# A four-layer image network on one core: the last image's norm by blocks under its own scans, and its inverse DFT and token layers in interleaved parts

## The chip, the cores and the metric

The kernel runs on one NeuronCore of a Trainium2 chip. The metric is device time in microseconds (us): 12547.97 us is the median of three runs (12536.14 to 12569.25). The profile comes from one further execution. A difference of 0.3% either way is about what counts as no change.

## The reference

The input is four images of 64 x 64 positions and 96 channels. Layer 0 is a 2D selective-scan block (four scan directions), layer 1 is the same kind of block applied to the image's real 2D DFT, with real and imaginary parts as 192 channels on 64 x 33 frequencies, and layers 2 and 3 are token layers: linear attention and a feed-forward part quantized to fp8.

```python
x = x + ss2d_0(group_norm(x))            # layer 0: 96 -> 192 channels
xf = rfft2(x); x = x + irfft2(ss2d_1(xf))  # layer 1: 192 -> 384 channels
t = tokens(x)                            # 4096 tokens of 96
for l in (2, 3):
    t = t + attn_l(layer_norm(t))        # (q k^T) v, without a softmax
    t = t + ffn_l(layer_norm(t))         # operands rounded to fp8 e5m2, sums to fp16
```

```python
def ss2d(x):
    xin, z = split(x @ in_proj.T)
    u = silu(depthwise_conv3x3(xin) + b)
    for k in range(4):                   # rows, columns, and both reversed
        dt, B, C = split(x_proj[k] @ u_k)
        delta = softplus(dt_proj[k] @ dt + bias)
        h = h * exp(delta * A) + delta * u_k * B     # along the sequence, 16 states
        y_k = sum_n(C * h) + D * u_k
    y = layer_norm(merge(y_0, y_1, y_2, y_3)) * silu(z)
    return y @ out_proj.T
```

## The kernel before

Channels lie on the 128 partitions in three chunks (C = 3). Layer 0 treats two images at a time (two "pairs" of half-width channels), layer 1 one image at a time. The scans are written in `scans`: six phases in a row (pair 0, pair 1, then layer 1 of images 0 to 3), in each the directions 0, 2, 1, 3, in each direction segments of the sequence. Layer 0 has 8 segments of 512 positions. Layer 1 has segments of 512, 512, 384, 384 and 320 positions, which are blocks of 8, 8, 6, 6 and 5 rows; directions 2 and 3 run through them from the last to the first. A segment is 12 steps: four groups of four states, times three channel chunks. A phase of layer 1 is so 240 steps, 96 of them 512 wide, 96 of 384 and 48 of 320; 1728 steps in all.

A step issues, in an order written out by hand: two exponentials on ScalarE (`ax`, L551), transposes of `bx` by TensorE (L546), four `tensor_tensor_scan` on VectorE (`hx`, `hy`, L576), products with C on GpSimd (`hcx`, L722) and on VectorE (`hcy`, L740), and transposing accumulations by TensorE (`acc`, L598). When the last group of a segment's chunk is through, `close_chunk` copies `acc` to SBUF (L625) and stores it to `y` in DRAM (L627), one step later. Rows of C and B are fetched by SyncE (SP) three steps ahead, as broadcasts (`bc`).

All other work is written as Python generators, "side" work. Each step has three slots; in a slot at most one generator is resumed up to its next `yield`, so a piece of its instructions goes into the engines' streams between those of the scan. `rate` of the phase (RATES) is the mean number of resumptions per step. A generator that yields LATE is only resumed in the third slot, before `hcy`. Work put off with `E.defer` (mostly the copy out of PSUM) is issued at the next slot. In the scans the side work has one PSUM buffer (`ms`).

The side lists: pair 1's preparation under phase 0; norm and out_proj of pair 0 with DFT and projection of images 0 and 1 under phase 1, and so on; `end1` of image b (norm, out_proj, inverse DFT, token layers) under the scans of image b + 1. `end1` of image 3 runs alone after the scans (`alone`, four PSUM buffers), outside of the hand-written order. What a list has left over goes on into the next phase; what is left after the last step is run by `E.finish`.

The parts of `end1`:

- `gated`: by blocks of rows, loads `y` of all directions (`yt`, L300, L304) and `u` (`ut`, L306), two rows at a time, merges and transposes them in PSUM (`py`, L327, L333), takes means and variances by matmuls (`pm` L347, `pv` L357), scales, multiplies with the gate and projects (`out1`, `po` L831), storing `att`.
- `inverse`: three groups of 32 channels in a row. Each loads `at` (L912), does 128 matmuls `piv` (L920, L921) and their copies to `v`, then 16 matmuls `pio` (L934), adds the image and stores `x1` (L940).
- `tokens`: loads all tokens (`tok`, L960) and the layer's weights, then a pipelined `layer_norm` over all tokens, the Gram matrix `pg` (L1036) and a chain of small matmuls, attention in 8 groups of four token columns (`pt` L1057, `pao` L1063), `layer_norm`, and the feed-forward in 8 groups (`ptf` L1072, `ph` L1080, `h16` and `h8` L1081 to L1087, `pfo` L1092, y16 L1100 to L1106). `h16`, `h8` and `y16` have one buffer.

Of the kernel before, what the change touches and what calls it, by code (L numbers as in the profile page):

```python
# [6 lines left out]
F32 = mybir.dt.float32  # L7
F16 = mybir.dt.float16
F8 = mybir.dt.float8e5
AF = mybir.ActivationFunctionType  # L10
# [15 lines left out]
RATES = [1.4, 2.25, 2.47, 2.47, 2.47, 2.47]  # L26
# [30 lines left out]
class Env:  # L57
# [5 lines left out]
    def __init__(self, tc, psum):  # L63
        self.tc, self.nc, self.psum = tc, tc.nc, psum
        self.later, self.queue, self.done = [], [], set()
        self.key = self.task = self.wants = None
# [44 lines left out]
class Block:  # L111
# [171 lines left out]
    def gated(self, E, g, io, out_proj):  # L283
# [5 lines left out]
        with E.pool(f"{cfg.pre}nm{g}") as sp:  # L289
# [4 lines left out]
                (b, i, r + i, min(2, n - i)) for b, (r, n) in enumerate(cfg.rows) for i in range(0, n, 2)  # L294
# [14 lines left out]
            todo = iter(tiles)  # L309
            nxt = load(*next(todo))  # L310
            yield
            yield
            yield
            for b, (r, nr) in enumerate(cfg.rows):
                n = nr * 64
                nm = f"{cfg.pre}_{g}_{r}"
# [3 lines left out]
                for i in range(0, nr, 2):  # L320
                    m = min(2, nr - i) * 64
                    yt, ut = nxt
                    more = next(todo, None)
                    nxt = load(*more) if more else None
# [81 lines left out]
def scans(tc, ctx, phases, ident):  # L406
# [213 lines left out]
    def close_chunk(st):  # L620

        z, c = st.z, st.c
        y = sp.tile([P, NBK, P], F32, name=f"y_{st.nm}", tag="y", bufs=2)
        for lo, hi, n in z.runs:
            nc.scalar.copy(y[:n, lo:hi], z.acc[c][:n, lo:hi])  # L625
            t = z.a + lo * P
            nc.sync.dma_start(  # L627
                out=z.ph.io["y"][z.k % 2][z.k // 2, t : t + (hi - lo) * n, c * P : (c + 1) * P].rearrange(
                    "(b p) d -> p b d", p=n
                ),  # L630
                in_=y[:n, lo:hi],
            )
# [266 lines left out]

def inverse(E, cst, att, x, b, x1):  # L900

    nc = E.nc
    G = 32
    with E.pool(f"fi{b}") as sp:
# [4 lines left out]
        for c0 in range(0, CH, G):  # L909
            a = sp.tile([HH, WF, 2, G], F32, name=f"at_{b}_{c0}", tag="at")  # L910
# [4 lines left out]
            v = sp.tile([WF, G, 2, HH], F32, name=f"v_{b}_{c0}", tag="v")  # L915
# [10 lines left out]
            HC = 16  # L926
            for h0 in range(0, HH, HC):
                xr = sp.tile([WW, HC, G], F32, name=f"xr1_{b}_{c0}_{h0}", tag="xr", bufs=2)
# [13 lines left out]
                )  # L942
        yield
# [5 lines left out]
def tokens(E, ins, consts, ident, x1, b, out):  # L949


    nc = E.nc
    A = CH + 1
    with E.pool(f"tk{b}") as sp:
# [3 lines left out]
        nc.sync.dma_start(out=mask, in_=consts["head_mask"])  # L958
        x = sp.tile([P, NT, CH], F32, name=f"tok_{b}", tag="tok")
        nc.sync.dma_start(out=x, in_=x1.rearrange("(p t) c -> p t c", t=NT))  # L960
        xn = sp.tile([P, NT, A], F32, name=f"xn_{b}", tag="xn")
        nc.gpsimd.memset(xn[:, :, CH:A], 1.0)
        yield
        yield

        def layer_norm(nm):

            Q = 8
            parts = []

            def scale(part, ts):
                t0, v = part
                for t in ts:
                    nc.scalar.activation(xn[:, t0 + t, :CH], xn[:, t0 + t, :CH], AF.Copy, scale=v[:, t : t + 1])  # L974

            n = NT // Q
            for i in range(n + 2):
                yield LATE
                if 1 <= i <= n:
                    nc.vector.tensor_reduce(parts[i - 1][1], sq, AX.X, ALU.add)  # L980
                if i < n:
                    t0 = i * Q
                    s = sp.tile([P, 2, Q], F32, name=f"lns_{nm}_{t0}", tag="lns", bufs=3)
                    m = s[:, 0, :]
                    parts.append((t0, s[:, 1, :]))
                    xs, xq = x[:, t0 : t0 + Q, :], xn[:, t0 : t0 + Q, :CH]
                    nc.vector.tensor_reduce(m, xs, AX.X, ALU.add)
                    nc.vector.tensor_scalar(m, m, 1.0 / CH, None, ALU.mult)
                    nc.vector.tensor_tensor(
                        xq, xs, m.rearrange("p (t o) -> p t o", o=1).to_broadcast([P, Q, CH]), ALU.subtract  # L990
                    )
                if i >= 2:
                    scale(parts[i - 2], range(4, Q))
                if i == n + 1:
                    return
                yield
                if i < n:
                    sq = sp.tile([P, Q, CH], F32, name=f"lnq_{nm}_{t0}", tag="lnq", bufs=2)
                    nc.scalar.activation(sq, xq, AF.Square)
                if i >= 1:  # L1000
                    v = parts[i - 1][1]
                    nc.scalar.activation(v, v, AF.Ln, bias=eps, scale=1.0 / CH)
                    nc.scalar.activation(v, v, AF.Exp, scale=-0.5)
                    scale(parts[i - 1], range(4))
# [6 lines left out]

        for ly in (2, 3):
            nm = f"{b}_{ly}"
            wq = sp.tile([A, 3 * CH], F32, name=f"wqkv_{nm}", tag="wqkv")
            nc.sync.dma_start(out=wq, in_=ins[f"l{ly}_wqkv"])
            wqt = sp.tile([CH, A], F32, name=f"wqt_{nm}", tag="wqt")
            nc.sync.dma_start(out=wqt, in_=ins[f"l{ly}_wqt"])
            wff = sp.tile([CH, CH], F32, name=f"wff_{nm}", tag="wff")
            nc.sync.dma_start(out=wff, in_=ins[f"l{ly}_wff"])
            bff = sp.tile([A, CH], F32, name=f"bff_{nm}", tag="bff")  # L1020
            nc.sync.dma_start(out=bff, in_=ins[f"l{ly}_bff"])
            q = {}
            for name, shape in (("w1", [CH, 4 * CH]), ("w2", [P, 3, CH]), ("b1", [P, 3]), ("b2", [P, CH])):
                t = sp.tile(shape, F32, name=f"{name}_{nm}", tag=name)
                src = ins[f"l{ly}_{name}"]
                nc.sync.dma_start(out=t, in_=src.to_broadcast([P, CH]) if name == "b2" else src)
                q[name] = sp.tile(shape, F8, name=f"q{name}_{nm}", tag=f"q{name}")
                yield LATE
                nc.vector.tensor_copy(q[name], t, saturate=False)
                if name in ("b1", "b2"):  # L1030
                    nc.vector.tensor_copy(t, q[name])
                    q[name] = t
            yield from layer_norm(nm + "a")
# [15 lines left out]
            small(CH, mt, wff, f"pw_{nm}", lambda t: nc.scalar.copy(pw, t))  # L1049
            yield  # L1050
            wo = sp.tile([A, CH], F32, name=f"wo_{nm}", tag="wo")
            small(A, wqt, pw, f"pe_{nm}", lambda t: nc.vector.tensor_tensor(wo, t, bff, ALU.add))
            yield
            for g in range(NT // 4):
                pt = E.psum(f"pt_{nm}_{g}")[:A]
                for i in range(4):
                    nc.tensor.transpose(pt[:, i * P : (i + 1) * P], xn[:, g * 4 + i, :], ident)  # L1057
                xt = sp.tile([A, 512], F32, name=f"xt_{nm}_{g}", tag="xt", bufs=2)
                E.defer(lambda xt=xt, pt=pt: nc.scalar.copy(xt, pt))
                yield  # L1060
# [233 lines left out]
```

## Time and profile before

| what | us |
|---|---|
| median of three runs | 12547.97 |
| the profiled execution | 12570.44 |
| its span, first to last instruction | 12568.7 |
| start to first scan step's end | 531 |
| scans, six phases | 2505, 2621, 1548, 1559, 1636, 1586 |
| after the last scan step | 580 |

| engine | busy us | share of the span |
|---|---|---|
| VectorE (DVE) | 10484.0 | 83% |
| TensorE (PE) | 9890.4 | 79% |
| ScalarE (ACT) | 9119.7 | 73% |
| GpSimd (POOL) | 8877.6 | 71% |

The phases are taken from the start of the first `hcy` of each to that of the next. The shares are means over stretches with different limits, so the stretches are read one by one: a row of a windows view gives the start and end of a stretch, its length, each engine's busy time in it (with the number of instructions), the granted share of the TensorE clock, and the DMA's share and rate. A wait row gives an engine and instruction, what it waited for, total us, how often, and the longest.

### The profile page before, as it was taken

What the parts mean: (1) busy time and instruction counts of PE and PEld (TensorE: products, weight loads), DVE (VectorE), ACT (ScalarE), POOL (GpSimd) and SP (SyncE); (2) the same over time, 40 slices, a digit from 0 to 9 for tenths busy, and PEclk for the clock granted to TensorE, in tenths of its full rate; (3) what the DMA queues carried; (4) which work ended last, traced back from release to release, by engine and by line L of the source; (5) the groups of instructions that cost most, each with busy time, mean ns of one, the idle gap of its engine ahead of it and who ended that gap; (6) DMA issues with size and microseconds to landing.
All of it is one profiled execution on the core that took longest, in us unless ns stands there. A gap on an engine that the chain in (4) does not pass through costs nothing. (4 is left out here: it accounts for less than half of the span.)

```text
span 12568.7 us, 164814 instructions
## 1 busy us (share of the span) xinstructions
PE 9890.4 (79%) x54680; PEld 7002.8 (56%) x54680; DVE 10484.0 (83%) x10170; ACT 9119.7 (73%) x18624; POOL 8877.6 (71%) x7057
## 2 busy tenths in 40 slices
PE   4677777777788878778888788788778977888766
PEld 1355555555666556556665565555556555565544
DVE  1399999999999998998788888978989699897923
ACT  1488888888778888886667777766777577776723
POOL 0388889998878898887678777866668566675600
PEclk8789999998989998998889998988789788887875
DMA  4344444444555445445443443443234322442231
GB/s 122 107 131 124 125 123 127 125 123 123 150 147 121 126 129 129 130 124 149 142 122 116 126 118 124 145 113 97 82 107 141 88 87 82 140 120 83 82 85 26
DMA packets 1264705, 1464.40 MB, mean 117 GB/s; under 512 B 494243, under 2 KB 1027055, under 8 KB 1255143
## 3 DMA queue, kind: packets, MB, share of 16 engines
q1 hardware_dynamic: 1263847, 1453.85, 41.8%
q8 instruction: 430, 7.05, 0.2%
q14 instruction: 428, 3.51, 0.1%
HBM read 1217.05 MB, written 236.50 MB: 116 GB/s over the span
## 5 line engine op out<-in xcount | busy, mean ns | idle before, releaser
L569 POOL TENSOR_TENSOR hy_l<-du_l,bc_l 128x512 f32<-128x512 f32 (+2 forms) x3456 | 3956.2, 1165 | 2358.8 <-DVE hcy_l L740 1194.6
L722 POOL TENSOR_TENSOR hcx_l<-hx_l,bc_l 128x1024 f32<-128x1024 f32 (+2 forms) x1617 | 3525.5, 2180 | 250.0 <-DVE hx_l L576 217.2
L526 ACT ACTIVATE bx_l<-dut_l,bt_l 128x192 f32<-128x192 f32 (+2 forms) x6272 | 2770.9, 498 | 0.1
L598 PE MATMUL acc_l<-ident,hcy_l 128*128 128x128 f32 (+1 forms) x12006 | 1854.2, 303 | 395.5 <-DVE hcy_l L740 392.2
L598 PE MATMUL acc_l<-ident,hcx_l 128*128 128x128 f32 (+1 forms) x12006 | 1885.0, 306 | 327.5 <-POOL hcx_l L722 322.7
L551 ACT ACTIVATE ax_l<-delta_l,l_alog 128x512 f32<-128x512 f32 (+2 forms) x3456 | 2138.9, 666 | 0.0
L598 PEld LDWEIGHTS acc_l<-ident,hcy_l 128*128 128x128 f32 (+1 forms) x12006 | 1553.3, 156 | 928.6 <-DVE hcy_l L740 574.4
L598 PEld LDWEIGHTS acc_l<-ident,hcx_l 128*128 128x128 f32 (+1 forms) x12006 | 1541.1, 156 | 823.1 <-POOL hcx_l L722 598.8
L576 DVE TENSOR_TENSOR_SCAN hx_l<-ax_l,state_l,b_l 128x512 f32<-128x512 f32 (+2 forms) x1663 | 1804.2, 1126 | 218.9 <-PE b_l L546 136.8
L740 DVE TENSOR_TENSOR hcy_l<-hy_l,bc_l 128x1024 f32<-128x1024 f32 (+2 forms) x1617 | 1926.8, 1192 | 43.7
L576 DVE TENSOR_TENSOR_SCAN hy_l<-b_l,state_l,hy_l 128x512 f32<-128x512 f32 (+2 forms) x1664 | 1808.3, 1121 | 139.1 <-ACT b_l L551 119.8
L551 ACT ACTIVATE b_l<-delta_l,l_alog 128x512 f32<-128x512 f32 (+2 forms) x1928 | 1210.3, 628 | 820.2 <-DVE hx_l L576 774.3
L546 PE MATMUL b_l<-ident,bx_l 128*128 128x128 f32 (+1 forms) x6776 | 1208.4, 305 | 406.9 <-DVE hy_l L576 200.3
L551 ACT ACTIVATE ab_l<-delta_l,l_alog 128x512 f32<-128x512 f32 x1308 | 900.0, 688 | 664.8 <-DVE hx_l L576 622.1
L546 PEld LDWEIGHTS b_l<-ident,bx_l 128*128 128x128 f32 (+1 forms) x6776 | 838.0, 153 | 925.1 <-DVE hy_l L576 314.1
L576 DVE TENSOR_TENSOR_SCAN hy_l<-ab_l,state_l,hy_l 128x512 f32<-128x512 f32 x948 | 1160.2, 1259 | 74.2 <-ACT ab_l L551 71.5
L576 DVE TENSOR_TENSOR_SCAN hx_l<-ax_l,state_l,ab_l 128x512 f32<-128x512 f32 x949 | 1161.1, 1264 | 68.2 <-PE ab_l L546 27.1
L546 PE MATMUL ab_l<-ident,bx_l 128*128 128x128 f32 x5236 | 897.2, 307 | 380.3 <-DVE hy_l L576 177.2
L589 POOL COPY state_l<-hx_l 128x2 f32<-128x2 f32 x1344 | 1087.6, 809 | 0.0
L546 PEld LDWEIGHTS ab_l<-ident,bx_l 128*128 128x128 f32 x5236 | 650.4, 155 | 711.7 <-DVE hx_l L576 272.9
L244 PE MATMUL pc_l<-pad_l,l_dg 128*128 128x512 f32 (+2 forms) x1944 | 927.2, 577 | 83.5 <-ACT uh_l L233 73.8
L163 PE MATMUL pi_l<-xi_l,l_wi 96*128 96x384 f32 (+6 forms) x912 | 446.6, 674 | 280.0 <-DMA xi_l<-xn 136.4
(192 smaller groups left out, 12605.9 us busy)
## 6 DMA issues: line engine op xcount, KB each, us to landing
bc_l<-l_xd_l SPq DMA_DIRECT2D x1536, 256.0 KB
bc_l<-l_xd_l SPq DMA_DIRECT2D x384, 512.0 KB
bc_l<-l_xd_l SPq DMA_DIRECT2D x384, 384.0 KB
us_l<-l_u SPq DMA_DIRECT2D x96, 768.0 KB
l_y<-y_l SPq DMA_DIRECT2D x288, 256.0 KB
bc_l<-l_xd_l SPq DMA_DIRECT2D x192, 320.0 KB
yt_l<-l_y SPq DMA_DIRECT2D x264, 192.0 KB
yt_l<-l_y SPq DMA_DIRECT2D x128, 384.0 KB
```

The source lines that it names most:

```text
L163: self.nc.tensor.matmul(out[i * cfg.PI : (i + 1) * cfg.PI, :n], wi[:, ki, half, :], xin[:, max(i, ki), :n], start=(ki == 0), stop=(ki == c ...
L244: nc.tensor.matmul(pc[:, : n * 64].rearrange("p (r w) -> p r w", w=64), diag[:, t, :], pad[:, r - p0 + dy : r - p0 + dy + n, dx : dx + 64] ...
L526: nc.scalar.activation(t[:n, b, :, ch], z.dut[:n, b, :, ch], AF.Copy, scale=z.bt[:n, b, m : m + 1])
L546: nc.tensor.transpose(pb[:, t : t + n], st.z.bx[st.q, j][:n, b, st.c], ident[:n, :n])
L551: nc.scalar.activation(out, z.delta[:, st.c, : z.S], AF.Exp, scale=z.blk.A[:, st.c, z.k, n : n + 1])
L569: nc.gpsimd.tensor_tensor(st.hy[:, j, :S], st.z.du[:, st.c, :S], st.z.b[st.q][:, j, :S], ALU.mult)
L576: nc.vector.tensor_tensor_scan(h[:, j, : z.S][:, ::step], a[:, : z.S][:, ::step], b[:, : z.S][:, ::step], 0.0 if z.first else z.state[st.c ...
L589: copy(z.state[st.c][:, n0 : n0 + 2].rearrange("p (j o) -> p j o", o=1), h[:, :, e : e + 1])
L598: nc.tensor.matmul(z.acc[st.c][:n, b, :], hc[:, j, t : t + n], ident, start=(n0 + j == 0 and b == 0), stop=(n0 + j == NST - 1 and b == 0), ...
L722: nc.gpsimd.tensor_tensor(hcx[:, :, :S], hx[:, :, :S], z.c[q][0][:, :, :S], ALU.mult)
L740: nc.vector.tensor_tensor(hcy[:, :, :S], st.hy[:, :, :S], z.c[q][1][:, :, :S], ALU.mult)
```

## The change

Four things are changed.

- `gated` takes its blocks in a given order and asks `ready(b)` before it loads one. `norm1_last` is `gated` for image 3, blocks in reverse order, each ready when the last direction's three chunks of that segment are closed (`closed`, written by `close_chunk`). It is the last side task of the last phase.
- `end1` is split into `norm1` and the rest. In `alone`, with `wide=4` and eight PSUM buffers, `inverse` runs its three channel groups in turns (`together`), and `tokens` runs its norm, attention and feed-forward as four parts of eight token columns in turns, each part with its own buffers, up to its own store of the output. Under the scans `wide` is 1 and parts follow one another; the norms are by parts there too.
- The weights of both token layers are loaded ahead of the inverse DFT in `alone`.
- RATES rise from 2.25 to 2.45 in phase 1, from 2.47 to 2.85 in phases 2 to 4 and to 3.0 in phase 5.

```diff
-RATES = [1.4, 2.25, 2.47, 2.47, 2.47, 2.47]
+RATES = [1.4, 2.45, 2.85, 2.85, 2.85, 3.0]
...
-    def gated(self, E, g, io, out_proj):
+    def gated(self, E, g, io, out_proj, order=1, ready=lambda b: True):
...
-            for b, (r, nr) in enumerate(cfg.rows):
+            nxt = None
+            for b, (r, nr) in list(enumerate(cfg.rows))[::order]:
                 n = nr * 64
+                if nxt is None:
+                    while not ready(b):
+                        yield
+                    nxt = load(*tiles.pop(0))
+                    yield
+                    yield
+                    yield
...
-                    more = next(todo, None)
-                    nxt = load(*more) if more else None
+                    nxt = load(*tiles.pop(0)) if tiles and ready(tiles[0][0]) else None
...
     def close_chunk(st):
 
         z, c = st.z, st.c
+        z.ph.io["closed"].append((z.k, z.a))
...
+def together(tasks, width):
+
+    tasks, active = list(tasks), []
+    while tasks or active:
+        while tasks and len(active) < width:
+            active.append(tasks.pop(0))
+        for task in list(active):
+            try:
+                yield next(task)
+            except StopIteration:
+                active.remove(task)
...
 def inverse(E, cst, att, x, b, x1):
...
-        for c0 in range(0, CH, G):
-            a = sp.tile([HH, WF, 2, G], F32, name=f"at_{b}_{c0}", tag="at")
+        def channels(c0, w):
+            a = sp.tile([HH, WF, 2, G], F32, name=f"at_{b}_{c0}", tag=f"at{w}")
...
+        W = min(E.wide, CH // G)
+        yield from together([channels(c0, c0 // G % W) for c0 in range(0, CH, G)], W)
...
+        loads = [weights(ly) for ly in (2, 3)]
+        ws = [next(loads[0])] + ([next(loads[1])] if W > 1 else [])
+        yield
         x = sp.tile([P, NT, CH], F32, name=f"tok_{b}", tag="tok")
         nc.sync.dma_start(out=x, in_=x1.rearrange("(p t) c -> p t c", t=NT))
...
+        def layer_norm(nm, p):
+
+            t0, w = p * Q, p % W
+            yield LATE
+            s = sp.tile([P, 2, Q], F32, name=f"lns_{nm}_{p}", tag=f"lns{w}")
...
+        def part(ly, p, wo, q):
+            nm, w = f"{b}_{ly}", p % W
+            groups = range(p * Q // 4, (p + 1) * Q // 4)
+            for g in groups:
+                yield from attend(nm, g, w, wo)
+            yield from layer_norm(nm + "f", p)
+            for g in groups:
+                yield from feed(nm, g, w, q)
+            if ly == 2:
+                yield from layer_norm(f"{b}_3a", p)
+            else:
+                t = slice(p * Q, (p + 1) * Q)
+                nc.sync.dma_start(out=out[b].rearrange("(p t) c -> p t c", t=NT)[:, t], in_=x[:, t])
...
+        yield from together([layer_norm(f"{b}_2a", p) for p in parts], W)
...
+            yield from together([part(ly, p, wo, q) for p in parts], W)
...
+        def norm1_last(E, b):
...
+            yield from blk[1].gated(
+                E, b, io, lambda E, *a: put(E, blk[1], *a),
+                order=-1,
+                ready=lambda i: io["closed"].count((3, cfg.rows[i][0] * 64)) == C,
+            )
...
+        def end1(E, b):
+            first = tokens(E, ins, consts, ident, x1[b], b, out)
+            if E.wide > 1:
+                yield next(first)
+            yield from inverse(E, consts, single[b]["att"], x0[b], b, x1[b])
+            yield from first
...
-            with tc.tile_pool(name="aloneps", bufs=4, space=PSUM) as ps:
-                E = Env(tc, lambda name: ps.tile([P, 512], F32, name=name, tag="ps"))
+            with tc.tile_pool(name="aloneps", bufs=8, space=PSUM) as ps:
+                E = Env(tc, lambda name: ps.tile([P, 512], F32, name=name, tag="ps"), wide=4)
...
-            [(end1, 0)],
-            [(end1, 1)],
-            [(end1, 2)],
+            [(norm1, 0), (end1, 0)],
+            [(norm1, 1), (end1, 1)],
+            [(norm1, 2), (end1, 2), (norm1_last, 3)],
```

## The prediction

> **What bounds the kernel now.** I read the page's span and slices first, then the chain of waits for its long pieces after the last scan, then windows of that end, and last windows of scan stretches picked by which side work runs in them.
>
> ```profile
> span 12568.7 us, 164814 instructions
> ...
> PE   4677777777788878778888788788778977888766
> ...
> DVE  1399999999999998998788888978989699897923
> ...
> PEclk8789999998989998998889998988789788887875
> ```
>
> (The DVE row is the scans' engine; each digit is a slice of 314 us.) The program has three stretches. Up to 531 us image pair 0 is prepared alone. From 531 to 11989 us the scans run with side work between their instructions: VectorE (DVE) is busy 10276 of 11456 us. From 11989 us to the end nothing is scanned. That end:
>
> ```profile
> core 0: us, PE busy (x) PEld busy (x) DVE busy (x) ACT busy (x) POOL busy (x), PEclk, DMA share, GB/s
> 11989.00:12025.00 36.00, 16.00 (x78) 7.82 (x77) 15.48 (x29) 9.96 (x18) 0.00 (x0) 0.52 0.30 93
> 12025.00:12215.00 190.00, 129.33 (x578) 92.61 (x576) 28.40 (x51) 29.47 (x52) 0.00 (x0) 0.76 0.38 104
> 12215.00:12347.00 132.00, 123.64 (x432) 76.54 (x432) 7.47 (x11) 13.94 (x25) 0.00 (x0) 0.52 0.23 37
> 12347.00:12569.00 222.00, 121.98 (x641) 87.75 (x640) 115.49 (x210) 97.22 (x262) 0.16 (x1) 0.55 0.06 21
> ```
>
> These 580 us are: a rest of image 2's tokens, image 3's norm and out_proj (190), its inverse DFT (132), its tokens (222). In the inverse PE is busy 124 of 132 us: it is bound by PE. In the tokens no engine is above 55%: they are bound by latency. Two waits say where:
>
> ```profile
> PE pfo L1092 <- DVE h L1087: 39.1, 16, 3.0
> ...
> ACT xt L1059 <- PE pt L1057: 32.2, 16, 3.0
> ```
>
> Scan stretches, 24 steps each (12 in the fourth; the count is that of the hcy/cy products of L740): 512 columns with no side work; 512 with norm and out_proj; 384 with the same; 384 with token feed; 384 with inverse; 512 and 384 with inverse.
>
> ```profile
> 2880.20:3036.50 156.30, 112.72 (x633) 85.29 (x633) 147.97 (x123) 126.75 (x262) 126.39 (x87) 0.85 0.40 104
> 11002.60:11163.00 160.40, 131.60 (x795) 100.03 (x794) 156.60 (x141) 122.85 (x219) 128.23 (x86) 0.88 0.41 128
> 10861.70:11002.60 140.90, 116.05 (x700) 83.52 (x698) 127.59 (x141) 106.56 (x217) 105.05 (x99) 0.90 0.51 148
> 8947.30:9022.30 75.00, 53.82 (x318) 39.90 (x316) 70.11 (x89) 54.67 (x113) 48.06 (x49) 0.82 0.26 80
> 8392.90:8574.10 181.20, 166.98 (x811) 105.63 (x809) 122.54 (x132) 106.86 (x217) 102.32 (x99) 0.77 0.37 96
> 11163.00:11348.10 185.10, 176.22 (x971) 119.79 (x971) 149.64 (x131) 122.19 (x226) 134.06 (x99) 0.84 0.40 104
> ```
>
> Per step: 6.51, 6.68, 5.87, 6.25, 7.55, 7.71 us. At 512 the DVE is the bound and norm work hides almost wholly. At 384 the scans alone need 4 x 0.995 + 0.946 = 4.93 us of DVE (form rows), so about 5.13 with the 0.2 us that the first stretch has above its own DVE sum (6.51 - 4 x 1.26 - 1.27); there side work is paid. Inverse work makes PE the bound at any width (busy 92 to 95%).
>
> [...]in the inverse PE works without gaps for 28 us at a time and is granted 0.52. So I don't credit denser PE work with a faster clock. [...]at 11990.06 us PE stands 0.99 us for a copy of h on ACT, with later matmuls behind. [...]The trace has 2.80 us from the att store to the first att load (chain of waits).
>
> **The change part by part.**
>
> *Norm by blocks under the last direction (norm1_last).* A turn is one resumption of a side generator. By the code a block of rows takes 28 (5 rows), 29 (6) or 35 turns (8), and 3 more to await its first load. Direction 3 of the last image closes its segments in the order of blocks 4, 3, 2, 1, 0, every 12 steps, and a step has three slots: 36 turns. So blocks 4, 3, 2 fit, block 1 misses by some 8 turns, block 0 comes after the last scan. Of the first two windows (226 us) there remains: the last y store and its landing, 2.9 us (last acc copy 11988.94, first y load issued 11991.84), one load of 4.4 us (ut loads in the chain: 5.73, 4.35, 4.24, 4.47), block 0 itself, 45 us (first py 12030.4, last po 12065.86 + 9.61), and 4 us because it now runs with the scans' one spare PSUM buffer in place of four (four out_proj tiles, each with a 0.47 us copy and a handoff in series). 56 us. Block 1's rest lies under the landing and the load. Saved: 170.
>
> *Inverse in three parts.* The chain has per part 28.2 us of piv and 14.0 of pio, gapless, at half clock. Interleaving removes the gaps (132 - 124 = 8) and delays the start, as six att loads come before PE's first round instead of two (one pair 3.3 us; I take 6). The 17 weight and mask DMAs stand ahead of the att store on SP at 0.3 to 0.6 us of issue, but block 0's compute hides them; without that cover 7 us. 131 us: saved 1.
>
> *Tokens in four parts.* Before: 9 us from the last x1 add to the loaded x; 28.5 to the end of the first norm, Gram matrix and small chain (12357.1 to 12385.6); attend 28.5; feed 55.5 (one pfo group each 6.9 us, since h16, h8 and y16 have one buffer); 16 to layer 3's attend; 28.5; 54; 2. Sum 222. After: 9. The first norm 27 (weights are there, but with four parts in step ACT's squares and scales come in one batch). Attend is bound by PE, 8 x (1.06 + 2.02) = 25. Feed has a DVE sum of 0.68 + 3 x 0.35 + 0.96 + 0.56 + 0.55 = 3.8 a group, PE 1.05 + 1.46 + 1.14 = 3.65: 30, and 7 to fill. The norm between attend and feed, hidden before, shows for 5, and the norm between layers no longer hides in the feed: 14 + 7 = 21. 9 + 27 + 67 + 21 + 67 + 2 = 193: saved 29. Bounds: 150 (DVE's 115 busy, the x load, a first norm) and 222.
>
> The end thus goes from 580 to 56 + 131 + 193 = 380: -200.
>
> *Cost in the scans.* No work is removed there; four blocks and 31 turns of image 2's tokens (the first window) move in. Two blocks fall at 384: 58 turns x (5.87 - 5.13) / 2.38 (57 turns in those 24 steps, by the code) = 18. Two at 512: 64 x (6.68 - 6.51) / 2.4 = 5. The 31 feed turns: (6.25 - 5.13) / 2 (turns a step) = 0.56 each, 17. The new y loads can't come before the y store has landed, and only three turns (one step, 6 us) lie between load and first matmul, against 2.9 + 4.4 us: PE waits some 3 us in each of four blocks, with the scans' transposes queued behind: 12. SP's bc fetches, queued behind the same loads, are a quarter-segment (3 steps) early and keep that cover. Higher rates (2.25 to 2.45, 2.47 to 2.85 and 3.0) squeeze the same work into fewer steps; where PE or DVE is the bound the sum is the same, and at 384 and 320 columns I add 18 for stretches that leave the balance. The token norms have more turns (20 for 11) and the same instructions: 0. Sum +70. Bounds: 0, as in the last four phases DVE idles 887 of 6329 us and could take it all, and +200.
>
> *Eight PSUM buffers for the first stretch:* PE waits there for xi loads (130.8 us), never for a buffer: 0.
>
> Total: -200 + 70 = -130. The profiled execution took 12570.4 us, so 12440; the median shown is 22 us below it: 12418.
>
> **Rivals.** *A, the above: 12418.* *B, the token parts overlap down to DVE's sum (150) and the scans swallow the rest (+20):* 56 + 131 + 150 = 337, -243 + 20, 12325. For it: DVE's idle time. Against: parts in step want the same engine at once. *C, the parts of the end don't overlap (PE at half clock sets inverse and attend, tokens stay 222):* 170 + 1 - 70 = -101, 12447. For it: PE busy 124 of 132. *D, slower: the waits of side matmuls in PE's order.* With nearly every slot filled, each narrow step (144 of 240 in four phases, 576) gets dearer; from 0.35 us a step (200 / 576) the end's gain is gone, and at 0.45 it is +259 - 200 = +59, 12607. For it: norm work at 384 already costs 0.74 us a step with no engine full. Against: at 2.4 turns a step four of five slots are filled already. *E, half of that (+160):* 12508.
>
> **Chances.** A 0.52 (12365 to 12475), B 0.16 (12290 to 12365), C 0.10, E 0.11 (12475 to 12560), D 0.11. Within 0.3% (12510 to 12586) is about what a measurement of this kernel can't tell from no change. Faster: 0.52 + 0.16 + 0.10 + 0.04 of E = 0.82; same 0.07; slower 0.11. The range 12295 to 12510 leaves out D, E's upper part and the lowest B.
>
> **What would show it.** After the last scan some 380 us, in them no second block of py; the inverse still some 131 at a clock near 0.5; pfo groups every 3.8 us; the scans' stretch 11455 + 70. A scan stretch longer by over 200, or an inverse at full clock (about 70), would make it wrong.

## The result, and the profile after

| | before | after |
|---|---|---|
| median of ten runs, us | 12546.59 (12535.55 to 12569.25) | 12629.76 (12579.56 to 12659.88) |
| ratio, 95% interval | | 1.0063 (1.0048 to 1.0079) |
| profiled execution, us | 12570.44 | 12659.88 |
| start to the first scan step's end | 531 | 534 |
| scans, six phases | 2505, 2621, 1548, 1559, 1636, 1586 | 2501, 2673, 1641, 1600, 1657, 1689 |
| sum of the phases | 11455 | 11761 |
| from the last `hcy` to the end | 582 | 364 |

The kernel became slower by 0.6%, where 12418 was predicted. The end gained 219 us, close to the predicted 200. The scans lost 306 us; the prediction had 70. Both profiled executions lie 24 to 30 us above their medians, so the difference of the two (89 us) is about that of the medians (83 us).

The page of the changed kernel, its span and slices, which answer to those shown of before:

```profile
span 12658.1 us, 164731 instructions
...
PE   4677777777788788878888888897789777887777
...
DVE  1399999999998989998778798968888889769883
...
PEclk8789999989889889988779899867788778767786
```

In the right half of the PEclk row (20 slices of some 316 us, mostly layer 1) eleven digits are six or seven, where four were before. The mean granted clock of the six phases was 0.91, 0.91, 0.85, 0.87, 0.82, 0.83 before and is 0.91, 0.89, 0.83, 0.83, 0.81, 0.79 after: it is lower in each phase that lost time. The records of the clock in the two traces have no other values than 0.5 and 1 (0.5 for 3556 us in 386 stretches before, for 3971 us in 417 after), so a mean such as 0.83 says how long it stood at each.

Windows of the new end: the norm's rest, the inverse, the tokens.

```profile
core 0: us, PE busy (x) PEld busy (x) DVE busy (x) ACT busy (x) POOL busy (x), PEclk, DMA share, GB/s
12297.00:12352.00 55.00, 36.42 (x171) 24.27 (x170) 8.42 (x21) 8.28 (x15) 0.00 (x0) 0.84 0.36 91
12352.00:12484.00 132.00, 123.55 (x432) 75.70 (x432) 7.83 (x12) 14.20 (x25) 0.00 (x0) 0.51 0.23 39
12484.00:12658.00 174.00, 92.53 (x640) 69.94 (x640) 107.45 (x197) 94.48 (x262) 0.00 (x0) 0.68 0.06 20
```

55, 132 and 174 us stand where the prediction had 56, 131 and 193. The second row says what the inverse is bound by: PE is busy 124 of 132 us at a clock of 0.51 (0.52 before).

Now the place of the loss. I divided the scans by the side work that runs under them, from the order of the generator's turns in the code, and took from each stretch what its steps cost with no side work: 6.51 us at 512 columns and 5.13 at 384 as in the prediction, 4.40 at 320. (As a check: in a run below 54 steps at the end of the last phase have no side work; they took 299 us where these floors give 304.) What is left is called the excess of a stretch.

| side work | excess before, us | after |
|---|---|---|
| token layers | 377 | 473 |
| inverse DFT | 216 | 286 |
| forward DFT | 79 | 129 |
| norm and out_proj, layer 0 | 224 | 248 |
| norm and out_proj, layer 1 | 127 | 162 |
| projection | 120 | 150 |

Every kind of side work got dearer, also those to which nothing was added (the DFTs and the projection). The sharpest case is image 2's inverse under image 3's scans. Windows over it, before (33 steps) and after (27 steps):

```profile
11157.16:11406.97 249.81, 235.92 (x1243) 155.77 (x1244) 196.84 (x181) 161.26 (x303) 173.80 (x136) 0.82 0.38 101
```

```profile
10960.51:11235.62 275.11, 265.50 (x984) 153.19 (x984) 127.46 (x152) 119.13 (x253) 103.92 (x109) 0.57 0.28 66
```

There are fewer steps, and narrower ones, and 259 fewer matmuls, yet PE is busy 30 us longer, for 97% of the stretch. The clock fell from 0.82 to 0.57. Over its floors the stretch takes 148 us where it took 46. A matmul keeps PE 270 ns in the mean, before 190. Both stretches hold the same 384 `piv` and 48 `pio`, so part of this is their larger share among the rest; the runs below separate the two.

### The profile page after: what moved, and what is told of

It is laid out like the page before. It is cut to its first block, busy times and chain, and to the rows that moved or that the text cites. A ratio compares the mean times of both kernels' runs of the same rounds, so it can differ in the third digit from the quotient of the medians.

```text
span 12658.1 us, 164731 instructions
## 1 busy us (share of the span) xinstructions
PE 10038.6 (79%) x54680; PEld 7129.9 (56%) x54680; DVE 10484.4 (83%) x10170; ACT 9113.9 (72%) x18623; POOL 8851.1 (70%) x7058
## 5 line engine op out<-in xcount | busy, mean ns | idle before, releaser
L603 PE MATMUL acc_l<-ident,hcx_l 128*128 128x128 f32 (+1 forms) x11946 | 1911.8, 310 | 312.5 <-POOL hcx_l L728 308.0
L603 PEld LDWEIGHTS acc_l<-ident,hcx_l 128*128 128x128 f32 (+1 forms) x11946 | 1572.5, 159 | 802.3 <-POOL hcx_l L728 558.7
L551 PE MATMUL b_l<-ident,bx_l 128*128 128x128 f32 x6716 | 1222.1, 312 | 387.6 <-DVE hy_l L581 197.6
L551 PEld LDWEIGHTS b_l<-ident,bx_l 128*128 128x128 f32 x6716 | 860.6, 157 | 894.3 <-DVE hy_l L581 328.3
```

The costliest lines, as they stand in the source:

```text
L551: nc.tensor.transpose(pb[:, t : t + n], st.z.bx[st.q, j][:n, b, st.c], ident[:n, :n])
L603: nc.tensor.matmul(z.acc[st.c][:n, b, :], hc[:, j, t : t + n], ident, start=(n0 + j == 0 and b == 0), stop=(n0 + j == NST - 1 and b == 0), ...
```

## The experiments

Three theories were set against each other, and the expectations use these numbers. *Theory 1, density:* with the higher RATES more of PE's work in a step is thin DFT matmuls (operands on 64 of the 128 partitions, or fewer), the granted clock falls, and PE becomes the bound. *Theory 2:* the token layers written in parts cost more under the scans. *Theory 3:* the waits of `norm1_last` for its y loads hold up the scans. In the tables scans and end come from the profiled execution, the ratio from all runs against the kernel before on the same chip. Its median there was 12552 to 12559, where it was 12547 beside the changed kernel; what a run gains on the changed kernel's 12630, given below as the plain difference of the medians, is so some 6 to 12 us more.

| run | median, us | ratio, 95% interval | scans | end |
|---|---|---|---|---|
| before, new RATES only | 12762.23 | 1.0162 (1.0145 to 1.018) | 11645 | 545 |
| before, new end only | 12527.91 | 0.9972 (0.9961 to 0.9984) | 11450 | 554 |
| changed, old token code under the scans | 12592.36 | 1.0023 (1.0014 to 1.0032) | 11708 | 364 |
| changed, inverse on 128 rows | 12469.77 | 0.9934 (0.9921 to 0.9947) | 11633 | 309 |
| changed, 128 rows, same count | 12517.17 | 0.9968 (0.9957 to 0.998) | 11657 | 326 |

**New RATES only.**

```
-RATES = [1.4, 2.25, 2.47, 2.47, 2.47, 2.47]
+RATES = [1.4, 2.45, 2.85, 2.85, 2.85, 3.0]
```

> The kernel before with the new RATES alone; nothing is moved. Theory 1 (density): denser turns fill PE with the thin matmuls of the DFTs, the granted clock falls, and PE becomes the bound of the narrow steps. Then the scans get longer by 130 to 200 us (before 11455, after 11761), the rest of image 2's tokens (36 us) moves in, and the time is 12640 to 12710. Theory 2 (the norms of the token layers, written part by part, cost their extra turns under the scans) and theory 3 (norm1_last's waits on y hold PE's queue): the rates are innocent, the scans stay within 30 us and the time is 12510 to 12545.

Measured: 12762, 204 us slower than before, more than the 80 to 150 that theory 1 gave. One line, with nothing added, costs more than the whole change does. The end got 37 us shorter, as a rest of image 2's tokens is now done under the scans, and the scans 190 us longer. By side work, 94 of the 190 lie in the inverse (216 to 310; its three stretches' clocks went from 0.81, 0.72, 0.82 to 0.69, 0.74, 0.60) and 48 in the forward DFT (79 to 127; the clock of its later stretches fell from 0.83 and 0.84 to 0.71 and 0.68). The inverse's third stretch, to be held against the two rows shown above:

```profile
10906.93:11171.05 264.12, 252.33 (x978) 146.34 (x976) 125.61 (x151) 116.85 (x251) 99.90 (x107) 0.60 0.28 67
```

And the `piv` alone, 384 in each of the three stretches with inverse work: the sum of the stretches, then busy times, before and with the new RATES:

```profile
sum 757.71, PE 180.19 PEld 132.00 ACT 41.52; mean PE 60.06 PEld 44.00 ACT 13.84
```

```profile
sum 757.65, PE 208.00 PEld 145.04 ACT 41.53; mean PE 69.33 PEld 48.35 ACT 13.84
```

The same 1152 matmuls keep PE 180 us before and 208 here. The RATES also shift the places of the side work: the third inverse falls on narrower steps than before, the second on wider ones, and the second's clock did not fall. Over all three the steps have nearly the same mean width (416 columns before, 409 here), so the places alone don't explain the sum.

**New end only.** The scans as before, with the old RATES and the old token code; image 3's norm runs after them, then the inverse and the tokens in parts.

```
-            [(norm1, 2), (end1, 2), (norm1_last, 3)],
+            [(norm1, 2), (end1, 2)],
...
-        alone(end1, 3)
+        alone(norm_end, 3)
```

> The scans and all side work under them as in the kernel before (old RATES, old token code under the scans, image 3's norm after the scans), and only the end in interleaved parts with the weights ahead. All theories: the scans stay at 11455 and the end loses what it lost in the changed kernel, tokens 222 to 174 and nothing else: 12500. If the time is not within 20 of that, the end's gain depends on what runs before it.

Measured: 12528, 30 less than before; the expected 12500 was missed by 28. The scans stayed at 11450, and the tokens take 174 us (221 before), as in the changed kernel. But from the last `po` to the first `piv` 23 us pass, where 7 passed before: SP issues the token weights (L995) there, ahead of the `at` loads, and no block's work hides them. From the last `po` to the last `pio` it takes 148 us for 133. So to load the weights ahead costs about 16 us where nothing covers it (the prediction had 7 for that case), and the end's gain depends on what runs before it. That 30 is also the sum of two terms of the prediction (1 for the inverse, 29 for the tokens) is chance: the tokens gave 47, and the loads took 16 back.

**Old token code under the scans.** The changed kernel; images 0 to 2 use the token layers as they were, image 3's end the new parts.

```
-            first = tokens(E, ins, consts, ident, x1[b], b, out)
+            task = tokens if E.wide > 1 else tokens_scan
+            first = task(E, ins, consts, ident, x1[b], b, out)
```

> The changed kernel with the kernel before's token code for images 0 to 2 under the scans; all else, RATES too, as changed. Theory 1: only the tokens' own surplus goes (excess over the bare scans 473 us in the changed kernel, 377 before for somewhat fewer turns), so at most 60 us less: 12570 to 12630. Theory 2: the scans come back to some 11530 and the time to 12400.

Measured: 12592, 37 less than the changed kernel's 12630 (49 less when each is held against the kernel before beside it). Theory 2 has a share and isn't the main cause. The difference to the run of the RATES alone is `norm1_last` and the new end: the end lost 182 us and the scans gained 63. In the changed kernel's profile the 46 last steps, which carry `norm1_last`, have 25 us of excess in all, which leaves its waits little there. Theory 3 falls as the main cause too: the RATES cost 190 of the 306 us with nothing moved.

**Inverse on 128 rows.** The first stage of the inverse, `piv`, multiplies real and imaginary parts in two matmuls of 64 rows each. Stacked on the partitions they are one matmul on 128 rows.

```
-            a = sp.tile([HH, WF, 2, G], F32, name=f"at_{b}_{c0}", tag=f"at{w}")
+            a = sp.tile([2 * HH, WF, G], F32, name=f"at_{b}_{c0}", tag=f"at{w}")
...
-                    nc.tensor.matmul(o, a[:, :, 0, i0 + i], ih[:, 0, :], start=True, stop=False)
-                    nc.tensor.matmul(o, a[:, :, 1, i0 + i], ih[:, 1, :], start=False, stop=True)
+                    nc.tensor.matmul(o, a[:, :, i0 + i], ih, start=True, stop=True)
```

> The changed kernel with the inverse DFT's first stage as one matmul on 128 rows (real and imaginary parts stacked on the partitions) in place of two on 64 rows; the same output, the same turns, half as many piv matmuls. Theory 1: PE gets free in the inverse's stretches under the scans and keeps a higher clock there (0.57 to 0.82 in the changed kernel, over 0.8 here); of its 286 us of excess 150 to 200 go, and the inverse alone at the end falls from 132 to 90: 12390 to 12440. Theories 2 and 3: the inverse at the end falls all the same, but the scans lose only the matmuls' own share of the excess, under 80: 12510 to 12560.

Measured: 12470, 160 less than the changed kernel and faster than the kernel before. It lies between the ranges of the theories, nearer to that of theory 1. The inverse's excess under the scans is 151 instead of 286, so 135 less where theory 1 had 150 to 200, at clocks of 0.78 to 0.81. This run halves the number of matmuls too, so alone it can't tell the clock from the count.

**128 rows, same count.** Both matmuls are kept, each on 128 rows; the half of `ih` that doesn't belong to it is zero.

```
-        ih = sp.tile([HH, 2, 2 * HH], F32, name=f"ih_{b}", tag="ih")
-        nc.sync.dma_start(out=ih, in_=cst["ih"])
+        ih = sp.tile([2 * HH, 2, 2 * HH], F32, name=f"ih_{b}", tag="ih")
+        nc.gpsimd.memset(ih, 0.0)
+        for r in range(2):
+            nc.sync.dma_start(out=ih[r * HH : (r + 1) * HH, r, :], in_=cst["ih"][:, r, :])
...
-                    nc.tensor.matmul(o, a[:, :, 0, i0 + i], ih[:, 0, :], start=True, stop=False)
-                    nc.tensor.matmul(o, a[:, :, 1, i0 + i], ih[:, 1, :], start=False, stop=True)
+                    nc.tensor.matmul(o, a[:, :, i0 + i], ih[:, 0, :], start=True, stop=False)
+                    nc.tensor.matmul(o, a[:, :, i0 + i], ih[:, 1, :], start=False, stop=True)
```

> The changed kernel with the inverse's piv matmuls on 128 rows, but still two of them (real and imaginary parts stacked on the partitions, the other half of the constant zero): the same count of matmuls, the same columns, the same turns, the same output; only the rows that a matmul fills are doubled. If the granted clock follows how much of the array a matmul fills (theory 1): piv at the end runs at a clock near 0.8 and 145 ns each as in the run with half as many, so the end loses 25 us, and the stretches with inverse work under the scans lose about a half of what they lost there: 12520 to 12580. If only the number of matmuls counts: no change from the changed kernel, 12610 to 12650, with 0.50 and 216 ns.

Measured: 12517, 113 less than the changed kernel, with no matmul saved; 3 us below the expected range. The same work at the end, where nothing else runs on PE: a window over `piv` and the tile's own view, first of the changed kernel, then of this one.

```profile
12359.30:12442.40 83.10, 82.35 (x385) 66.51 (x386) 0.00 (x0) 13.32 (x23) 0.00 (x0) 0.50 0.16 25
```

```profile
L941 PE MATMUL piv<-ih,at x192: 414/414/423, 12360.7 to 12442.0; 64*33 64x128 f32 x192
```

```profile
12255.50:12299.70 44.20, 44.13 (x385) 43.07 (x385) 0.00 (x0) 13.32 (x23) 0.00 (x0) 0.96 0.26 41
```

```profile
L943 PE MATMUL piv<-ih,at x192: 272/273/418, 12255.9 to 12299.5; 128*33 128x128 f32 x192
```

(The tile's view gives shortest, median and longest duration in ns, then the operands' partitions and columns.) Both windows hold 384 matmuls with less than 1 us of gaps. On 64 rows they go at a clock of 0.50, one per 216 ns; on 128 rows at 0.96, one per 115 ns. So in this pair the clock follows how many rows the matmuls fill; count and gaps are the same. (The stacked operand also lies otherwise in SBUF. An edit of the forward DFT, below, leaves that as it is, and there the clock goes from 0.68 to 0.93.) More gaps stand beside a lower clock too, though these two runs differ in the count as well: in the run with half as many matmuls PE is idle 2.0 of the 27.8 us of its `piv` at the end, at a mean clock of 0.80, and in this run 0.1 of 44.2 us, at 0.96. If the clock was 0.5 or 1 there as in the two traces above, it stood at 0.5 for some 11 us in the one and some 4 us in the other (estimates from the two means). Under the scans the same edit gives, in the stretch shown above of the changed kernel at 0.57:

```profile
10922.94:11132.11 209.17, 198.94 (x984) 118.03 (x984) 126.61 (x151) 118.70 (x253) 104.47 (x109) 0.83 0.36 86
```

The same 27 steps and 984 matmuls take 209 us instead of 275, at 0.83. PE is busy 97% and 95% of them: it stays the bound of this stretch, and what changed is the price of its work. Over the three inverses the excess falls by 99 us of the 135 that half the count gave. The scans' own matmuls, which the edit doesn't touch, show it too. Two groups by form in this stretch, of the changed kernel and then of this one (busy us and mean ns after the bar):

```profile
L551 PE MATMUL _l<-ident,bx_l 128*128 128x128 f32 x140 | 37.4, 404 | 0.0
L603 PE MATMUL acc_l<-ident,cx_l 128*128 128x128 f32 x138 | 36.4, 398 | 0.0
```

```profile
L551 PE MATMUL _l<-ident,bx_l 128*128 128x128 f32 x140 | 29.3, 331 | 0.4 <-DVE hy_l L581 0.4
L603 PE MATMUL acc_l<-ident,cx_l 128*128 128x128 f32 x138 | 28.2, 326 | 0.0
```

A transpose of the scans lasts 404 ns beside thin matmuls and 331 beside full ones. Here the thin work taxes the work that it is mixed with.

**The square: RATES by thin or full matmuls.** The runs so far show that RATES cost time and that thin matmuls do. If the RATES cost through the thin matmuls, they must cost less where the inverse is "cured", that is, has its first stage on 128 rows. The kernel before with `piv` on 128 rows (the edit above), then the same with the new RATES, then with the forward DFT's first stage `pfz` on 128 rows at the same count:

```
-        fw = sp.tile([WW, 2 * WF], F32, name=f"fw_{b}", tag="fw")
-        nc.sync.dma_start(out=fw, in_=cst["fw"])
+        fw = sp.tile([2 * WW, 2 * WF], F32, name=f"fw_{b}", tag="fw")
+        nc.gpsimd.memset(fw, 0.0)
+        nc.sync.dma_start(out=fw[:WW], in_=cst["fw"])
+        xs = [sp.tile([2 * WW, HH, G], F32, name=f"xw_{b}_{k}", tag=f"xw{k}") for k in range(2)]
+        for t in xs:
+            nc.gpsimd.memset(t, 1.0)
...
+            t = xs[c0 // G % 2]
+            nc.sync.dma_start(out=t[:WW], in_=x.rearrange("(h w) c -> w h c", w=WW)[:, :, c0 : c0 + G])
```

> The kernel before with one edit: the inverse's first stage (piv) is one matmul on 128 rows instead of two on 64. Together with the kernel before, the run of the RATES alone and the next run it makes a square: old and new RATES, thin and full first stage. By the clock (theory 1) the inverse's excess over the bare scans falls from 216 to some 140 us, its clock rises to about 0.8, and the end loses some 45 us: about 12430. If the thin matmuls cost nothing under the scans at the old RATES (rival: their price is only in the order of the turns), only the end's 45 us go: about 12505.

> The previous kernel with the new RATES. Without the fuller matmuls the new RATES cost 204 us (12762 against 12558), of which 94 lay in the inverse under the scans. Theory 1, the clock: with the inverse cured the new RATES cost some 204 - 94 = 110 us over the previous kernel, and the inverse's excess is at most 160 where it was 310. The rival, that denser side work costs through the slots it takes and the order of PE's queue and not through the clock, expects the same 204 us again.

> The previous kernel with the forward DFT's first stage (pfz) on 128 rows too: the lower 64 rows are constants met by zero weights, so the count of matmuls stays. Theory 1: the clock of the forward DFT's stretches rises from about 0.7 to over 0.85 and their excess (127 us with the new RATES, 79 before) falls to about 85: some 40 us less than the previous kernel. The rival, that the price lies in the count of matmuls or in the second stage (two matmuls of 64 rows by 128 columns), expects no difference beyond 15 us.

| run | median, us | ratio, 95% interval | scans | end | excess inverse | forward |
|---|---|---|---|---|---|---|
| before, inverse on 128 rows | 12456.81 | 0.9921 (0.9908 to 0.9935) | 11410 | 525 | 159 | 81 |
| the same, new RATES | 12569.49 | 1.0008 (1.0 to 1.0017) | 11550 | 502 | 180 | 133 |
| the same, forward DFT on 128 rows too | 12524.44 | 0.9975 (0.9966 to 0.9984) | 11493 | 495 | 180 | 88 |

The new RATES cost 204 us with thin matmuls and 113 with the inverse cured; 110 was expected of theory 1, 204 of its rival. The inverse's excess rises by 21 where it rose by 94. Its 128-row `piv`, 192 in each of three stretches, don't get slower at all, with old and with new RATES:

```profile
sum 710.00, PE 99.92 PEld 62.18 ACT 41.24; mean PE 33.31 PEld 20.73 ACT 13.75
```

```profile
sum 638.71, PE 100.13 PEld 61.97 ACT 41.44; mean PE 33.38 PEld 20.66 ACT 13.81
```

They keep PE 99.9 and 100.1 us, where the thin ones went from 180 to 208. With the forward DFT cured as well another 45 us go. Its fourth stretch, in both runs with the same 607 matmuls, before and after that last edit:

```profile
7091.35:7208.39 117.04, 104.72 (x607) 84.11 (x605) 69.24 (x67) 69.10 (x139) 58.91 (x56) 0.68 0.50 110
```

```profile
7063.72:7162.60 98.88, 89.13 (x607) 73.20 (x605) 69.37 (x66) 69.12 (x138) 57.80 (x56) 0.93 0.60 124
```

DVE and ACT do the same to 0.2 us, POOL to 1.1; the clock goes from 0.68 to 0.93, and 18 us go. So 91 of the 204 us (204 - 113, by the intervals good to some 30) go through the inverse's thin first stage. They need not all be the clock's: this edit halves the count of `piv` too and so relieves PE, and the edit that keeps the count was run at the new RATES alone. The forward DFT's 45 us come with the count and the layout kept and with the clock, but that edit wasn't run at these old RATES, where it may gain something too. So 136 us (91 + 45) are an upper end for what goes through thin matmuls. The other 68 us at least are spread over norm, projection and token stretches; their cause was not tried and stays open.

The first run of the three missed: 12430 was expected for the old RATES, and it gave 12457, as the inverse's excess fell by 57 and not by 76.

**A middle RATE, and the best version.** With RATES of 2.6 instead of 2.85 (and 2.25 instead of 2.45 in phase 1):

```
-RATES = [1.4, 2.45, 2.85, 2.85, 2.85, 3.0]
+RATES = [1.4, 2.25, 2.6, 2.6, 2.6, 3.0]
```

| run | median, us | ratio, 95% interval | scans | end |
|---|---|---|---|---|
| changed, old token code, RATES 2.6 | 12448.72 | 0.9915 (0.9901 to 0.9928) | 11503 | 411 |
| the same, inverse on 128 rows | 12287.16 | 0.9796 (0.9781 to 0.9811) | 11396 | 351 |
| the same, forward DFT's second stage on 128 rows | 12289.39 | 0.9788 (0.9775 to 0.9802) | 11403 | 355 |
| the second, with the forward DFT's first stage on 128 rows | 12278.16 | 0.9784 (0.9769 to 0.9799) | 11389 | 355 |

> The changed kernel with the old token code under the scans and RATES [1.4, 2.25, 2.6, 2.6, 2.6, 3.0]; the inverse as it was. A third point between 2.47 (scans 11450) and 2.85 (11708, of which some 25 are norm1_last's). Theory 1 with a clock that falls gradually: scans about 11560, end 395, 12480 to 12530. If the clock tips over at some density: 11480 or 11700.

> Parts put together: norm1_last, the end in parts, old token code under the scans, the inverse's first stage as one matmul on 128 rows, and RATES [1.4, 2.25, 2.6, 2.6, 2.6, 3.0] between old and new. By these rates 75 turns are left after the last step in place of 45, about 30 us more in the end. Theory 1: the scans fall from 11633 (128 rows, new rates and token code) to 11450 to 11520; end 340; 12330 to 12400.

> As the run put together, with the forward DFT's second stage on 128 rows too (real parts on partitions 0 to 63, imaginary ones on 64 to 127, one matmul in place of two). Its stretches under the scans have an excess of 129 us in the changed kernel and 79 before, at clocks of 0.68 to 0.92. Theory 1: 40 to 70 us less than without: 12270 to 12350.

> The fastest version so far (12287) with the forward DFT's first stage (pfz) on 128 rows at the same count of matmuls, as in the previous run. There it took 45 us off at the new RATES. At these lower RATES the forward DFT has 105 us of excess over the bare scans at clocks of 0.92, 0.94, 0.81 and 0.74; theory 1 expects the last two stretches to come to over 0.85 and 20 to 30 us to go: 12257 to 12267. That the earlier edit of the forward DFT (its second stage on 128 rows, its first stage left on 64 and in twice as many matmuls) changed nothing would then be because it left the thin stage thin. If the result stays at 12287, the clock of these stretches isn't what the time hangs on at these RATES.

The middle RATES give a third point, with the old token code under the scans in all three: the scans take 11450 us at 2.47 (the run of the new end only), 11503 at 2.6 and 11708 at 2.85. By phases this is clearer, since other rates change along. Phases 2 to 4 take 4733 us at 2.47, 4733 at 2.6 and 4871 at 2.85, at mean clocks of 0.85, 0.85 and 0.83: the first step up costs nothing, the next, with twice the increase, 138. Phase 1 takes 2636 and 2628 at 2.25 and 2685 at 2.45. Phase 5 takes 1582 at 2.47 without `norm1_last`, 1643 and 1648 at 3.0 with it. Over these three points the cost is convex in the rate. This comes nearer to the clock that tips over (scans of 11480) than to the one that falls gradually (11560); both runs came out faster than expected, 12449 for 12480 to 12530 and 12287 for 12330 to 12400. With 2.6 the version with the old token code is 144 us faster than with 2.85, though 47 us more is left for the end.

With the inverse on 128 rows 12287 us is reached, 2% less than before. The forward DFT added nothing that stands out at these RATES. Its second stage alone was a miss (+2 us, 40 to 70 less had been expected): that edit had to keep the first stage on 64 rows, in twice as many matmuls. The first stage on 128 rows raised the clocks of the late stretches as expected (0.81 to 0.87, 0.74 to 0.91), and their kind's excess fell from 105 to 82; other stretches gave most of it back, and the 9 us of the medians are within the intervals, where 20 to 30 had been expected. The page of the version at 12287, against the first of before:

```profile
span 12280.8 us, 163259 instructions
...
PE 9664.3 (79%) x53912; PEld 6822.7 (56%) x53912; DVE 10472.9 (85%) x10170; ACT 9108.4 (74%) x18623; POOL 8850.7 (72%) x7058
```

DVE, ACT and POOL do what they did to 0.3%; PE has 226 us less (9664 us busy, before 9890). The span is 288 us shorter.

## Why the prediction was wrong

**The end (−200): right, in part by luck.** It came to 364 us for 380. The norm's rest is 55 (56), the inverse 132 (131), the tokens 174 (193). Inside the tokens the terms were off both ways. Windows of layer 2's attention in its 8 groups, before and after:

```profile
12385.60:12414.00 28.40, 23.02 (x96) 20.31 (x97) 12.75 (x20) 11.59 (x30) 0.00 (x0) 0.50 0.01 5
```

```profile
12517.50:12528.30 10.80, 10.66 (x97) 10.50 (x95) 5.00 (x10) 4.10 (x8) 0.00 (x0) 1.00 0.01 2
```

The prediction priced attend at 25 us a layer, from durations at a clock of 0.50. In parts PE does the same matmuls with 0.1 us of gaps, where it had 5.4 in layer 2, and is granted 1.00 in layer 2 and 0.86 in layer 3: 11 us and 12. That is 27 us less than counted, and other terms took 8 of them back; from attend to the feed, for one, 13 us pass where 5 were allowed. The chain of waits (start, length, what) shows one more miss:

```profile
12314.59 1.84 SPq L995
12317.32 4.14 SPq L995
12322.45 3.11 DMA b<-in_l_b
```

L995 is the DMA of the token weights. The prediction let block 0's work hide them and had 7 us for the case without cover; here the chain runs through SP's issue (6 us in the two pieces shown) and a load. The detour is short all the same: PE's `pm` matmuls of block 0 end beside it at 12324.38 us, and DVE goes on with the block at 12325.95.

**The norm's blocks under the last direction (+23, and +12 for PE's waits): right in size, as far as the excess shows it.** The steps that carry them have 25 us of excess.

**The token norms' extra turns (0): too low.** The old token code gives 37 to 49 us back (53 in the scans of the profiles). The prediction counted the same instructions and took the 9 more turns as free; which part of the new token code costs it wasn't separated.

**Higher rates (+18): the step that failed.** "Where PE or DVE is the bound the sum is the same" holds only if PE's work has a fixed price. RATES alone cost 190 us in the scans and 204 in time. By the square 91 of these go through the inverse's thin first stage, and up to 45 more through the forward DFT's. In the inverse's stretches, where PE is busy 92 to 97%, the same thin matmuls in fewer steps met a lower clock: the same `piv` kept PE 208 us instead of 180. The scans' own transposes and accumulations, too, are slower beside thin matmuls (404 ns, against 331 beside full ones). How the 91 us divide between this slower pace and PE's time in the steps that were left without side work isn't shown, and 68 us at least stay open. The bound of +200 for the scans was too low, in the main for the same reason. By the profiles, +306 is RATES 190, the blocks with the new end's weights and buffers 63, the token code 53. (These are single executions, and such a sum can be some 30 us off: the run of the RATES alone was profiled in the fastest of its four executions, and the changed kernel in the slowest of its ten.)

**The reading that led there.** The prediction had seen the low clock in the inverse at the end: 0.52, with PE working without gaps for 28 us at a time. From this one stretch it credited no faster clock anywhere, which was right for the inverse (0.51) and wrong for attend (1.00), and stopped there. It should have asked what a lower clock does to the scans when more of that work lies among them. Its own windows held a hint: 0.77 in the stretch at 384 columns with inverse work, 0.90 in that with norm work. The measurement decides: 83 us of thin matmuls with 0.8 us of gaps stayed at 0.50, and as many matmuls on 128 rows, with 0.1 us of gaps in 44 us, had 0.96. In attend, with operands on 97 to 128 rows, PE was busy 23.0 of 28.4 us at 0.50 before and 10.7 of 10.8 us at 1.00 after.

**The rivals.** D had the sign and the place, narrow steps with PE as their bound, and a threshold of 0.35 us a step that was passed (306 us over 576 steps would be 0.53). Its mechanism, waits of side matmuls in PE's order, is not what the runs with an equal count show: there the matmuls' own pace changed, at the same order. For the 68 us that stay open it wasn't tested. B and C, which speak of the end, were tested by the end: the token parts went some four tenths of the way from A's 193 to B's 150 (174), and the inverse was as A had it.

**The signs named beforehand.** No second block of `py` after the last scan and the inverse near 131 at about 0.5 came, and the end was near 380 (364). The `pfo` groups didn't come every 3.8 us but four in a burst, with the next burst 14.2 us later in layer 2, so 3.6 us a group. "A scan stretch longer by over 200" was named as what would make it wrong, and did.

## What to carry to other kernels

Before you make background work denser, look at the granted clock of the stretches where it runs: here PE was the bound of the inverse's stretch (busy 97%), its clock was 0.57 where it had been 0.82, and the foreground's matmuls went down with the side work's (a transpose of the scans took 404 ns beside thin matmuls and 331 beside full ones). Try fuller rows first (real and imaginary parts stacked, even with half of the products zero: 115 ns a matmul for 216 here), then choose the rate, and take three points of it: here the step from 2.47 to 2.6 cost phases 2 to 4 nothing and that from 2.6 to 2.85 cost them 138 us. Padding may bring nothing that can be measured: with the forward DFT at 2.6 it gave 9 us, within the intervals. And run such a rate by itself: here its loss and the end's gain of 219 us were in one change.

## What the runs showed of the hardware

- 384 fp32 matmuls in a row with 64 rows and 33 columns of stationary operand ran at a clock of 0.50 (216 ns each), with 128 rows and half of the products zero at 0.96 (115 ns each). More rows, even useless ones, cost less time here.
- With operands on 97 to 128 rows the clock went with the gaps: layer 2's attend (some 96 matmuls) took 28.4 us at 0.50 with 5.4 us of waits between its groups, and 10.8 us at 1.00 with 0.1 us.
- The clock was lower where thin matmuls were mixed with full ones: 0.57 in 275 us of scans with the inverse, 0.83 in 209 us with the same number of matmuls when `piv` was on 128 rows; the scans' own transposes took 404 and 331 ns there.
- The changed kernel's ten runs spread over 80 us (before 34), and their time went with the clock: 12579.56 us at a mean of 0.852, 12659.88 at 0.843.
